# Last layer's values as seven block products over pairs of contexts and pairs of head groups

## The chip, the cores and the metric

One core of a Trainium2 chip runs the whole kernel in one launch. Its engines work side by side, each through its own queue in order: TensorE (PE; PEld is its weight load), VectorE (DVE), ScalarE (ACT), GpSimd (POOL), and SyncE (SP), which issues nearly all transfers (DMAs). The metric is the device time of a launch in microseconds, the median of several executions. All data are float32, and a matmul in float32 shows as two matmul instructions ("passes") in the profile.

## The reference

Four layers run over x [8, 112, 512] with a context ctx [8, 375, 512]: one plain cross-attention, two RWKV layers of 32 heads of 16 channels, and a last layer of two cross-attentions and an MLP. What matters here, shortened:

```python
# layers 1 and 2, time mix (then a channel mix)
def step(s, (r_t, k_t, v_t, w_t)):
    a = k_t[..., :, None] * v_t[..., None, :]
    out = einsum('bhi,bhij->bhj', r_t, u * a + s)
    return a + w_t[..., :, None] * s, out
y = scan(step, s0, (r, k, v, w))
m, va = mean and variance of y over each head's 16 channels
x = x + (((y - m) / sqrt(va + 1e-5)) * gn_w + gn_b) * g @ Wo.T
...
# layer 3, twice (i = 1, 2), H = 16 heads of K = 128, t = 375 positions
h  = layer_norm(x)
qh = (h @ wq + bq).reshape(b, 112, H, K)
kh = concat[(ctx @ wk + bk).reshape(b, t, H, K), bias_k]   # 376 positions
vh = concat[(ctx @ wv + bv).reshape(b, t, H, K), bias_v]
p  = softmax(einsum('bqhk,bthk->bhqt', qh, kh) / sqrt(K))
x  = x + einsum('bhqt,bthk->bqhk', p, vh).reshape(b, 112, H * K) @ wo + bo
```

The keys and values of layer 3 depend on the context alone, not on x, so they can be computed at any time.

## The kernel before

The 16 heads of layer 3 are four groups of four heads, so a group's weight is a 512 x 512 matrix (four chunks k of 128 input channels). "Pieces" of work that depend on nothing near by are made by a Python generator, the filler; `fill(n)` takes n pieces of it and so puts their instructions at that place of the program.

**Values.** `values()` is that filler from layer 1 on. For each attention i, head group gr and context b it loads the context (L723, 750 KB) and multiplies its 375 positions, in chunks of 128, 128 and 119, with the group's weight: four matmuls of 512 columns into one PSUM bank (L751; two banks in all). ScalarE copies the result into one of three tiles `v` (L755) and a transfer stores it in DRAM, `vs` (L756). It yields after each two matmuls, so a piece is four passes. Layer 3 loads `vs` back (L961). There are 64 (i, gr, b) of 3 chunks of 4 matmuls of 2 passes, 1536 in all.

**Where the pieces stand.** In the layer norms of layers 1 and 2 (2, 2 and 4 in each half); 9 before the scans; in the scans one piece in steps 1, 5, 9 and 13 of 16, two in the others, 28 in all; 14 in the tail behind the scans; what is left over is taken in layer 3's first norm and before its first attention, where it is chained with the keys of the first pair of contexts (`first_keys`).

**The scans.** `time_mix` goes through 4 blocks of channels with 16 steps each, 64 in a layer, in an order that `manual_schedule` keeps as written for the engines. A step: `spread` starts a load of a row, spread over the partitions (`vj`, three ahead, L498); VectorE multiplies kv = vp * k in PSUM (L595); ScalarE copies the next `vj` to `vp` (`led`, L506 and L507); VectorE runs the recurrence over 904 elements (`st`, L598, three buffers); GpSimd multiplies rs = st * r (L602, eight buffers); TensorE sums rs into a bank `y` four steps at a time (`sums`, L576); then the pieces. `vp`, `kv` and `y` have one buffer each in PSUM. Beside the steps of one block runs the group norm of the block before, one operation a step: `take` adds y (L544) from step 3; for each half (448 columns) centring by a matmul (L519), square and copy on ScalarE (L522, L523), variance by a matmul (L526), square root (L529), reciprocal on VectorE (L531), products on GpSimd (L533, L539), from steps 4 and 8. Its two matmuls use the banks that the pieces use too.

**Keys.** `attention` computes the keys of layer 3 with seven products where the plain way takes eight (`seven`, matmuls at L794), over pairs of contexts and halves of a group's channels. The sums of contexts that this needs come from layer 0: `context_sums` makes them on GpSimd and stores them for each pair. The attention of a context then takes scores (L967), softmax, transposed probabilities (L970), and probabilities times values (L980, three chunks).

Of the kernel before, what the change touches and what calls it, by code (L numbers as in the profile page):

```python
# [30 lines left out]
P = 128  # L31
# [14 lines left out]
CHUNKS = [(0, 128), (128, 128), (256, T - 256)]  # L46
# [59 lines left out]
def tile_kernel(ctx: ExitStack, tc: tile.TileContext, d: dict, out: bass.AP):  # L106
# [53 lines left out]
    def layer_norm_half(ps, work, y, h, scale, offset, name, room=None, bank=None):  # L160
# [18 lines left out]
        fill(2)  # L179
# [3 lines left out]
        fill(2)  # L183
        var = over_channels(sq, "var")
        fill(4)
# [9 lines left out]
    def layer_norm(ps, work, dst, scale, offset, name, room=None, bank=None):  # L195


        for h in range(2):
            layer_norm_half(ps, work, halves(dst, h), h, scale, offset, name, room, bank)
# [13 lines left out]
    def layer0():  # L213
# [3 lines left out]
        CT = 125  # L217
        with (
# [18 lines left out]
            def context_sums(b, c1, c2):  # L237

                t = work.tile([P, 4, 2, S], F32, tag="sums", name=f"sums0_{b}", bufs=1)
                nc.gpsimd.tensor_sub(t[:, 0], c2[:, :2], c1[:, :2])  # L240
                nc.gpsimd.tensor_sub(t[:, 1], c2[:, 2:], t[:, 0])
                nc.gpsimd.tensor_sub(t[:, 2], c2[:, 2:], c2[:, :2])
                nc.gpsimd.tensor_sub(t[:, 3], c1[:, 2:], t[:, 1])
                to = shared["spill"].tile([P, 2, NC, S], F32, name=f"sums_{b // 2}")
                nc.sync.dma_start(to.rearrange("p a (b k) s -> p (a b) k s", k=2), t)
                shared["sums", b // 2] = to
# [34 lines left out]
            for b in range(B):  # L281
# [4 lines left out]
                if b % 2:  # L286
                    context_sums(b, cxs.pop(b - 1), cxs.pop(b))
# [39 lines left out]
    def rwkv(n, ones_t, center_h, pick, first, state0):  # L327
        pre, names = f"L{n}_xattn_", _RWKV[n]
        with tc.tile_pool(name=f"r{n}", bufs=1) as keep:
# [11 lines left out]
            def gates(name):  # L341
                return keep.tile([P, N], F32, tag="gate", name=name, bufs=2)

            time_mix_inputs(n, pre, names, ones_t, first, k, v, r, g, gates, decay, rows)
            time_mix(n, pre, center_h, pick, state0, k, v, r, g, gates, decay, rows)
        channel_mix(n, pre, names, first)

    def time_mix_inputs(n, pre, names, ones_t, first, k, v, r, g, gates, decay, rows):

        order = names["order"]  # L350
        with (
# [8 lines left out]
            w2e = one.tile([DM, C], F32, name=f"maa2e_{n}")  # L360
# [3 lines left out]
            d2 = one.tile([DD, C], F32, name=f"d2_{n}")  # L364
# [10 lines left out]
            for h in range(2):  # L375
                xa = one.tile([P, NC, NH], F32, tag="xa", name=f"xa{n}_{h}")
                sx = one.tile([P, NC, NH], F32, tag="sx", name=f"sx{n}_{h}")
                layer_norm_half(ps, work, xa, h, pre + "ln1_w", pre + "ln1_b", f"ln1_{n}")
# [3 lines left out]
                for c in range(NC):  # L382
                    nc.vector.scalar_tensor_tensor(
                        xx[:, c, :], sx[:, c, :], vec(pre + "maa_x", c), xa[:, c, :], ALU.mult, ALU.add
                    )
                t4 = one.tile([P, NH], F32, tag="t4", name=f"t4_{n}_{h}")
                t1 = one.tile([DM, NH], F32, tag="t1", name=f"t1_{n}_{h}")
                for dst, m0, m in ((t4, 0, P), (t1, P, DM)):
                    p = mm(ps, f"ps_t{n}_{h}_{m0}")[:m, :NH]
                    for c in range(NC):  # L390
                        nc.tensor.matmul(
                            p, w1[:, c, m0 : m0 + m], xx[:, c, :], start=c == 0, stop=c == NC - 1
                        )
                    nc.scalar.activation(dst, p, AF.Tanh)
# [18 lines left out]
                td = one.tile([DD, NH], F32, tag="td", name=f"td{n}_{h}")  # L413
# [13 lines left out]
                for f, dst, func in (  # L427
# [6 lines left out]
                    for o in range(NC):  # L434
# [5 lines left out]
                        if f == "g":  # L440
                            e = gates(f"g{n}_{o}_{h}")[:, :NH]
# [31 lines left out]
    def time_mix(n, pre, center_h, pick, state0, k, v, r, g, gates, decay, rows):  # L473
# [7 lines left out]
        ps = shared["ps"]  # L481
        mean_h = center_h[1]
        with (
            tc.tile_pool(name=f"s{n}", bufs=1) as one,
            tc.tile_pool(name=f"sw{n}", bufs=2) as work,
            tc.tile_pool(name=f"sv{n}", bufs=1, space=PSUM) as psv,
        ):
            y = v
            order = [4 * q + r for r in range(4) for q in range(4)]
# [3 lines left out]
            def spread(at):  # L493
                if at < len(steps):
                    c, j = steps[at]
                    vjs[c, j] = work.tile([P, N], F32, tag="vj", name=f"vj{n}_{c}_{j}", bufs=3)
# [13 lines left out]
            def gate(c):  # L510
                t = gates(f"gate{n}_{c}")
                nc.sync.dma_start(t, g[:, c, :])
                return t

            def group_norm(c, h, g):

                yh = halves(y[:, c, :], h)
                p = mm(ps, f"ps_gm{n}_{c}_{h}")[:, :NH]
                nc.tensor.matmul(p, center_h[0], yh, start=True, stop=True)  # L519
                yield  # L520
                sq = work.tile([P, NH], F32, tag="sq", name=f"gsq{n}_{c}_{h}")
                nc.scalar.activation(sq, p, AF.Square)  # L522
                nc.scalar.copy(yh, p)  # L523
                yield
                p = mm(ps, f"ps_gv{n}_{c}_{h}")[:, :NH]
                nc.tensor.matmul(p, mean_h, sq, start=True, stop=True)  # L526
                yield
                rstd = work.tile([P, NH], F32, tag="sq", name=f"grs{n}_{c}_{h}")
                nc.scalar.activation(rstd, p, AF.Sqrt, bias=eps)  # L529
                yield  # L530
                nc.vector.reciprocal(rstd, rstd)  # L531
                yield
                nc.gpsimd.tensor_mul(yh, yh, rstd)  # L533
                yield
                nc.scalar.activation(
                    yh, yh, AF.Identity, bias=gn[:, 1, c : c + 1], scale=gn[:, 0, c : c + 1]
                )
                yield
                nc.gpsimd.tensor_mul(yh, yh, halves(g, h))  # L539
# [7 lines left out]
            def beside(c):  # L547
# [4 lines left out]
                return {3: take(c - 1), 4: group_norm(c - 1, 0, g), 8: group_norm(c - 1, 1, g)}  # L552

            for at in range(3):
                spread(at)
            w_o = wpool.tile([P, NC, C], F32, tag="w", name=f"w_{pre}Wo")
            for q in range(4):
                nc.sync.dma_start(
                    w_o[32 * q : 32 * (q + 1)], turned_rows(d[pre + "Wo"].rearrange("p c n -> p (c n)"), q)
                )  # L560
            gn = one.tile([P, 2, NC], F32, name=f"gn{n}")
# [4 lines left out]
            fill(9)  # L566
            waiting, pys = [], {}

            def sums():

                for h in range(2):
                    for c, j, rs in waiting[:4]:
                        if c not in pys:
                            pys[c] = psv.tile([P, 2, 512], F32, tag="y", name=f"ps_y{n}_{c}")
# [12 lines left out]
            with tc.manual_schedule(engines=ORDERED):  # L587
                vp = led(0)
                for c in range(NC):
                    side = beside(c)  # L590
                    for at, j in enumerate(order):
# [3 lines left out]
                        nc.vector.tensor_mul(flat(kv), flat(vp), flat(k[:, c]))  # L595
                        vp = led(c * HS + at + 1)
                        st = work.tile([P, B, LP], F32, tag="st", name=f"st{n}_{c}_{j}", bufs=3)
# [3 lines left out]
                        rs = work.tile([P, N], F32, tag="rs", name=f"rs{n}_{c}_{j}", bufs=8)  # L601
                        nc.gpsimd.tensor_mul(by_batch(rs), st[:, :, :L], by_batch(r[:, c, :]))  # L602
                        waiting.append((c, j, rs))
                        if len(waiting) == 6:
                            sums()
                        fill(1 if at % 4 == 1 else 2)
# [7 lines left out]
            last = gate(NC - 1)  # L614
            last = [group_norm(NC - 1, h, last) for h in range(2)]
            for at in range(10):
                for h in range(2):
                    if at >= 2 * h:
                        next(last[h], None)
                fill(1)  # L620
# [7 lines left out]
    def channel_mix(n, pre, names, first):  # L628
        with (
# [4 lines left out]
            f_k, f_v, f_r = (weight(pre + names[f]) for f in ("Fk", "Fv", "Fr"))  # L634
            xc = one.tile([P, NC, N], F32, name=f"xc{n}")
            sx = one.tile([P, NC, N], F32, name=f"sxc{n}")
            layer_norm(ps, work, xc, pre + "ln2_w", pre + "ln2_b", f"ln2_{n}")
            shifted(sx, xc, first[:, 0])
# [542 lines left out]
```

## Time and profile before

| what | value |
|---|---|
| runs | 3078.76, 3079.95, 3086.07 us; median 3079.95 |
| profiled execution, its own time | 3069.73 us |
| its span, first to last instruction | 3068.0 us |
| mean granted TensorE clock | 0.991 |
| layers 0 and 1 up to the first kv of the scans | 375.46 us, PE busy 356.62 |
| layer 1's scans, 375.46 to 616.16 | 240.70 us, PE 233.27, DVE 220.56, ACT 113.62, POOL 133.38, DMA share 0.85 |
| tail, channel mix, up to layer 2's first kv at 1009.80 | 393.64 us, PE 384.61 |
| layer 2's scans, 1009.80 to 1249.10 | 239.30 us, PE 230.57, DVE 220.31, ACT 113.03, POOL 133.33, DMA share 0.87 |
| tail and channel mix of layer 2, to 1418.00 | 168.90 us, PE 163.85 |
| layer 3, from 1418.00 | 1650.00 us, PE 1611.45, DVE 911.46, DMA share 0.32 |

A row is a stretch of the profiled execution: how long it is and how long each engine was busy in it. Where an engine's busy time comes near the length, it sets the pace or works in step with the one that does. The DMA share is the mean busy share of the 16 DMA engines.

### The profile page before, as it was taken

The numbers are of one execution on the slowest core, as the hardware profiler recorded it, in microseconds if no ns is written. First come the engines' busy times: TensorE is split into PE (matmuls) and PEld (weight loads), VectorE is DVE, ScalarE is ACT, GpSimd is POOL, SyncE is SP. The second block draws the span as 40 slices with busy tenths as digits, with TensorE's granted clock in tenths as the row PEclk, the third lists the DMA queues.
The fourth block names the chain that finished last, engine by engine and source line by source line (L and its number), as shares of the span: only waits on it lengthen the run. The fifth ranks groups of instructions, "written<-read, shape, count | busy, mean of one in ns | idle before, by whom it ended". The sixth has DMA issues, their size and how long they took to land.

```text
span 3068.0 us, 28497 instructions
## 1 busy us (share of the span) xinstructions
PE 2980.4 (97%) x10098; PEld 1575.5 (51%) x10098; DVE 1641.4 (54%) x2432; ACT 812.5 (26%) x1675; POOL 647.3 (21%) x578
## 2 busy tenths in 40 slices
PE   9999999999999999999999999999999999999999
PEld 5634433344444333444366565656566665656544
DVE  1433289933332799454146564655756565645555
ACT  2122245422221444222122121212222221312311
POOL 2222255511322455212000101020001001010030
PEclk9999999999999999999999999999999999999999
DMA  5221398731121888323243342424323343422110
GB/s 226 85 87 61 123 299 252 234 111 65 53 73 66 264 276 259 115 75 116 101 138 131 116 137 96 146 94 137 112 100 125 115 138 104 149 93 91 48 55 24
DMA packets 113149, 390.29 MB, mean 127 GB/s; under 512 B 13112, under 2 KB 20952, under 8 KB 104688
## 3 DMA queue, kind: packets, MB, share of 16 engines
q1 hardware_dynamic: 113008, 388.48, 38.1%
q8 instruction: 80, 1.31, 0.2%
q14 instruction: 61, 0.50, 0.1%
HBM read 320.27 MB, written 68.16 MB: 127 GB/s over the span
## 4 chain that ended last, share of the span: by engine, by line
PE 59%; DVE 4%; issue 1%; DMA 1%; ACT 1%; POOL 0%; SPq 0%; DVEq 0%; ACTq 0%; POOLq 0%
PE ps_v L751 8%; PE av L980 5%; PE ps_k5k L794 5%; PE sc L967 5%; PE ps_k7k L794 5%; PE ps_k1k L794 5%; PE ps_k6k L794 3%; PE pt L970 2%; PE ps_k7q L794 2%; PE ps_k5q L794 2%; PE ps_o L155 2%; PE ps_k7o L794 1%; PE ps_k1q L794 1%; PE ps_k5fc L794 1%; PE ps_k5o L794 1%; PE ps_k7fc L794 1%
## 5 line engine op out<-in xcount | busy, mean ns | idle before, releaser
L751 PE MATMUL ps_v<-wv,cxv 128*128 128x512 f32 (+1 forms) x1536 | 686.6, 599 | 20.3 <-DMA cxv<-in_ctxT 12.4
L751 PEld LDWEIGHTS ps_v<-wv,cxv 128*128 128x128 f32 (+1 forms) x1536 | 284.8, 189 | 406.5 <-issue 371.3
L207 ACT ACTIVATE prob<-sc,top 112x376 f32<-112x376 f32 (+1 forms) x264 | 151.6, 575 | 666.4 <-DVE top L204 543.4
L602 POOL TENSOR_TENSOR rs<-st,r 128x896 f32<-128x896 f32 x128 | 246.6, 1926 | 244.6 <-DVE st L598 193.1
L598 DVE TENSOR_TENSOR_SCAN st<-decay,kv 128x904 f32<-128x904 f32 x128 | 260.7, 2037 | 13.3 <-DVE kv L595 0.5
L967 PE MATMUL sc<-k,q 128*112 128x376 f32 x512 | 202.2, 487 | 3.2 <-ACT q L927 2.4
L980 PEld LDWEIGHTS av<-pts,v 128*128 128x128 f32 (+1 forms) x1536 | 184.8, 193 | 31.2 <-DVE pts L976 16.0
L980 PE MATMUL av<-pts,v 128*128 128x112 f32 (+1 forms) x1536 | 188.7, 277 | 1.6 <-DMA v<-vs 1.6
L794 PE MATMUL ps_k1k<-cx,w_L_xattn_wk 128*128 128x375 f32 x512 | 186.1, 479 | 1.6 <-ACT rstdk L812 1.6
L755 ACT COPY v<-ps_v 128x512 f32<-128x512 f32 (+1 forms) x192 | 111.9, 583 | 259.3 <-PE ps_v L751 234.1
L595 DVE TENSOR_TENSOR kv<-vp,k 128x904 f32<-128x904 f32 x128 | 141.5, 1105 | 60.1 <-ACT vp L507 48.0
L958 POOL COPY k<-vecs 128x4 f32<-128x4 f32 x64 | 12.4, 201 | 742.9 <-PE sc L967 662.1
L204 DVE TENSOR_REDUCE top<-sc 112x1 f32<-112x376 f32 (+1 forms) x264 | 143.5, 544 | 29.2 <-PE sc L967 15.5
L794 PEld LDWEIGHTS ps_k1k<-cx,w_L_xattn_wk 128*128 128x128 f32 x512 | 95.1, 190 | 62.8 <-issue 2.0
L507 ACT COPY vp<-vj 128x896 f32<-128x896 f32 x128 | 116.5, 910 | 35.6 <-DMA vj<-rows 32.0
L209 DVE TENSOR_SCALAR prob<-prob,total 112x376 f32<-112x376 f32 (+1 forms) x264 | 121.2, 462 | 7.7 <-PE ps_k1k L794 0.5
L970 PEld LDWEIGHTS pt<-ident,prob 112*128 112x128 f32 (+1 forms) x768 | 84.7, 140 | 72.1 <-DVE prob L209 44.2
L970 PE MATMUL pt<-ident,prob 112*128 112x112 f32 (+1 forms) x768 | 110.2, 264 | 4.2 <-DVE prob L209 3.5
L987 DVE TENSOR_TENSOR ctxt<-av,bv 128x448 f32<-128x448 f32 x64 | 40.0, 624 | 127.7 <-PE av L980 127.6
L967 PEld LDWEIGHTS sc<-k,q 128*112 128x112 f32 x512 | 78.9, 176 | 44.3 <-ACT prob L207 6.8
L822 DVE TENSOR_TENSOR u2k<-ps_k6k,rstdk 128x375 f32<-128x375 f32 x64 | 35.0, 546 | 121.3 <-PE ps_k6k L794 121.2
L794 PE MATMUL ps_k7k<-cs,wsk 128*128 128x375 f32 x256 | 94.4, 481 | 0.9 <-DVE k L889 0.9
(349 smaller groups left out, 4434.0 us busy)
## 6 DMA issues: line engine op xcount, KB each, us to landing
vj<-rows SPq DMA_DIRECT2D x128, 448.0 KB
cxv<-in_ctxT SPq DMA_DIRECT2D x64, 750.0 KB
cs<-sums SPq DMA_DIRECT2D x64, 750.0 KB
vs<-v SPq DMA_DIRECT2D x128, 256.0 KB
v<-vs SPq DMA_DIRECT2D x64, 512.0 KB
cx<-in_ctxT SPq DMA_DIRECT2D x40, 750.0 KB
vs<-v SPq DMA_DIRECT2D x64, 238.0 KB
v<-vs SPq DMA_DIRECT2D x64, 238.0 KB
```

Of the source, the lines that this page charges most:

```text
L204: nc.vector.tensor_reduce(top, scores, AX.X, ALU.max, negate=True)
L207: nc.scalar.activation(prob, scores, AF.Exp, bias=top, accum_out=total)
L209: nc.vector.tensor_scalar(prob, prob, total, None, ALU.mult)
L507: nc.scalar.copy(vp[:, :, 1:], by_batch(vjs.pop((c, j))))
L595: nc.vector.tensor_mul(flat(kv), flat(vp), flat(k[:, c]))
L598: nc.vector.tensor_tensor_scan(flat(st), flat(decay[:, c]), flat(kv), 0.0, ALU.mult, ALU.add)
L602: nc.gpsimd.tensor_mul(by_batch(rs), st[:, :, :L], by_batch(r[:, c, :]))
L751: nc.tensor.matmul(p, cx[:, k, t0 : t0 + m], w_v[:, k, :], start=k == 0, stop=k == NC - 1)
L794: nc.tensor.matmul(p, lhsT, right[:, k], start=start and k == 0, stop=k == 1, skip_group_check=not start)
L967: nc.tensor.matmul(sc, q[:, o, tok], kt[:, o, :], start=True, stop=True)
L970: nc.tensor.transpose(pt[t][:nt, o, :], prob[:, t0 : t0 + nt], ident[:L, :L])
L980: nc.tensor.matmul(av[:, o, :], v[:nt, t, o * HD : (o + 1) * HD], pts[:nt, t, o, :], start=t == 0, stop=t == 2,)
```

## The change

The values are made by seven products of 256 input channels where the plain way takes eight. With a pair of contexts (positions of one chunk) and a pair of head groups, the context has blocks c11, c21 (halves of the channels of the first) and c12, c22 (of the second), the weights a11, a12 (halves for the first group) and a21, a22. The products are k1 = a11 c11, k2 = a12 c21, k6 = s1 t1, k7 = s2 t2, k8 = a22 t3, k5 = (a21 + a22) t0 and k9 = s3 c22, with sums t of the contexts and s of the weights; k1 + k2, k1 + k6 + k7 + k8, k1 + k6 + k7 + k5 and k1 + k6 + k5 + k9 are the four results.

**Chained in a bank.** k6, k7 and k8 are added to k1 in its PSUM bank, and ScalarE copies the bank out after each of the four; k2 has the other bank and is added to k1 by GpSimd; k5 and k9 are chained in the other bank in the middle of the next unit, and VectorE adds them (`last_two`). A unit (one chunk of 125 positions of a pair) has the order k1, k5 and k6, k9 and k7, k2, k8, with k5 and k9 of the unit before. There are four sets (i, pair of groups) of 12 units, and a fifth set of 3 units that makes keys: groups 1 and 2 of the first attention for the first pair of contexts, stored in DRAM and loaded in `key_pieces`. One product, four passes of 512 columns (16 of 125 for keys), is a piece.

```diff
-CHUNKS = [(0, 128), (128, 128), (256, T - 256)]
+CT = S // 3
+CHUNKS = [(0, CT), (CT, CT), (2 * CT, CT + 1)]
+BLOCKS = 7
+UNITS = B // 2 * 3
...
+        sets = [("wv", i, (gr, gr + 1)) for i in (1, 2) for gr in (0, 2)] + [("wk", 1, (1, 2))]
+        units = [(at, unit) for at in range(len(sets)) for unit in range(UNITS if at < 4 else 3)]
+        def tile_of(name):
+            return pool.tile([P, C], F32, tag="v", name=name, bufs=6)
...
+        def block(at):
+            m = at // 2
+            if m + 4 not in tiles:
+                load(m + 4)
+            return tiles[m][:, at % 2]
...
+        def last_two(u, f, u2, u3, s, at):
+            p = bank(u, f, f"k5_{u}")
+            product(p, block(at), s["k5"])
+            nc.vector.tensor_add(u3, p, u3)
+            store(u3, u, 1, 1)
+            yield "k5"
+            product(p, block(at + 2), s["k9"], start=False)
+            nc.vector.tensor_add(u2, p, u2)
+            store(u2, u, 0, 1)
+            yield "k9"
...
+            for what, n in (("k1", 0), ("k6", 2), ("k7", 4)):
+                product(first, block(base + n), s[what], start=not n)
+                kept.append(shaped(tile_of(f"{what}_{u}"), f))
+                nc.scalar.copy(kept[-1], first)
+                after(what)
+                yield
+                if n < 4:
+                    yield from late()
+            p1, u2, u3 = kept
+            p = bank(u + 1, f, f"k2_{u}")
+            product(p, block(base + 5), s["k2"])
+            y = shaped(pool.tile([P, C], F32, tag="k2", name=f"k2_{u}"), f)
+            nc.scalar.copy(y, p)
+            nc.gpsimd.tensor_add(p1, y, p1)
+            store(p1, u, 0, 0)
+            after("k2")
+            yield
+            product(first, block(base + 6), s["k8"], start=False)
+            y = shaped(tile_of(f"k8_{u}"), f)
+            nc.scalar.copy(y, first)
+            store(y, u, 1, 0)
+            after("k8")
+            yield
+            before = last_two(u, f, u2, u3, s, base + BLOCKS + 1)
```

**Blocks and weights.** Layer 0's `park` takes the place of `context_sums`: it makes the seven blocks of each pair and chunk (ScalarE copies three, GpSimd makes four sums) and stores them in DRAM in the order in which they will be read. `block` loads them two at a time, four loads ahead, into five tiles. `weights` loads a set's four blocks and makes the three sums on GpSimd; for three of the sets `relay` does this piece by piece in the last two units of the set before, each tile when its last use is past. The keys of layer 3 load their context sums from the same blocks.

**In the scans.** Two pieces a step, one of them before `vp`, but only one in steps 6 and 10 (30 in 16 steps); `st` has two buffers, `rs` six; the first two `vj` have a place of their own (`early`). The group norm works on both halves at once in the banks of `y`, its reciprocals come in four parts, `take` at step 2, centring at 3, variance at 4, reciprocals at 5, 6, 9 and 10. Pieces in the norms: none in the first half of layer 1's, two fewer in the second half of the channel mixes', three more after `xx`; 8 before the scans; in the tail 4 and then 5 in layer 1, 4 and 11 in layer 2; after the channel mix's norm 7 in layer 1 and all that are left in layer 2.

```diff
                         nc.vector.tensor_mul(flat(kv), flat(vp), flat(k[:, c]))
+                        fill(1)
                         vp = led(c * HS + at + 1)
-                        st = work.tile([P, B, LP], F32, tag="st", name=f"st{n}_{c}_{j}", bufs=3)
+                        st = work.tile([P, B, LP], F32, tag="st", name=f"st{n}_{c}_{j}", bufs=2)
...
                         waiting.append((c, j, rs))
+                        fill(int(at not in (6, 10)))
                         if len(waiting) == 6:
                             sums()
-                        fill(1 if at % 4 == 1 else 2)
...
             layer_norm(ps, work, xc, pre + "ln2_w", pre + "ln2_b", f"ln2_{n}")
+            fill(7 if n == 1 else 1000)
```

**Layer 3.** The pools of the values are closed before it, and its own are opened. The filler of its norms is the keys of the first pair alone. The keys are left without their bias, which shifts all scores of a query alike, except that the bias position's key becomes bias_k - bk (`over`). The values' tiles have 126 rows, 125 positions and the bias. State and small constants of the RWKV layers are loaded where they are used, and two small weights share a tile.

```diff
-        filler = chain(filler, first_keys())
+        filler = first_keys()
...
+            if ("wk", i, gr, b) in shared:
+                for j in range(2):
+                    kts.append(kv.tile([P, HG, T], F32, tag="kt", name=f"k{u}_{j}", bufs=3))
+                    for t in range(3):
+                        y = shared["wk", i, gr, b + j][:, t]
+                        nc.sync.dma_start(kts[-1][:, :, t * CT : (t + 1) * CT], y)
+                return
...
-                nc.gpsimd.tensor_copy(kt[:, :, S], vecs[:, at : at + HG])
+                nc.gpsimd.tensor_copy(kt[:, :, S], over[:, gr * HG : (gr + 1) * HG])
```

## The prediction

> **What bounds the kernel now.** I read the page's busy times, its slices and its costliest groups first, then windows cut at the 16-step blocks of the scans, then the vector and tensor timelines inside them.
>
> ```profile
> PE 2980.4 (97%) x10098; PEld 1575.5 (51%) x10098; DVE 1641.4 (54%) x2432; ACT 812.5 (26%) x1675; POOL 647.3 (21%) x578
> ...
> PE   9999999999999999999999999999999999999999
> ...
> DVE  1433289933332799454146564655756565645555
> ...
> DMA  5221398731121888323243342424323343422110
> ...
> L751 PE MATMUL ps_v<-wv,cxv 128*128 128x512 f32 (+1 forms) x1536 | 686.6, 599 | 20.3 <-DMA cxv<-in_ctxT 12.4
> ```
>
> TensorE is busy in every slice; only 3068.0 - 2980.4 = 87.6 us of the span are idle. So a removed matmul pass is worth its time wherever something else doesn't take over. One thing nearly does: in slices 5 to 7 and 13 to 15, the two scans, VectorE is at 8 or 9 tenths too, and so is the DMA.
>
> ```profile
> 446.30:507.70 61.40, 60.34 (x189) 24.31 (x188) 56.83 (x36) 30.72 (x56) 35.22 (x20) 1.00 0.81 242
> 507.70:567.40 59.70, 57.18 (x180) 22.53 (x178) 56.69 (x36) 27.90 (x52) 35.19 (x20) 1.00 0.84 258
> ...
> 1009.80:1079.80 70.00, 65.84 (x196) 26.12 (x195) 62.73 (x40) 30.72 (x58) 36.57 (x19) 0.98 0.96 290
> ```
>
> Columns: length, busy PE, PEld, DVE, ACT, POOL, granted clock, DMA share, GB/s. A block of 16 steps takes 59.7 to 61.4 us with VectorE busy 56.7: two engines are full at once.
>
> ```profile
> 487.80 1.11 DVE L595 TENSOR_TENSOR kv<-vp,k 128x904 f32<-128x904 f32 x1
> 489.01 2.04 DVE L598 TENSOR_TENSOR_SCAN st<-decay,kv 128x904 f32<-128x904 f32 x1
> 491.15 1.11 DVE L595 TENSOR_TENSOR kv<-vp,k 128x904 f32<-128x904 f32 x1
> ...
> 505.77 2.04 DVE L598 TENSOR_TENSOR_SCAN st<-decay,kv 128x904 f32<-128x904 f32 x1
> 507.73 1.06 DVE L544 TENSOR_TENSOR v<-ps_y,v 128x896 f32<-128x896 f32 x1
> 508.71 1.10 DVE L595 TENSOR_TENSOR kv<-vp,k 128x904 f32<-128x904 f32 x1
> ...
> 525.27 2.93 DVE L531 RECIPROCAL grs<-grs 128x448 f32<-128x448 f32 x1
> 528.12 1.08 DVE L595 TENSOR_TENSOR kv<-vp,k 128x904 f32<-128x904 f32 x1
> ```
>
> A bare step is 491.15 - 487.80 = 3.35 us: 1.11 + 2.04 and two gaps of 0.1, because each instruction needs the one before. What is slipped in between fills such a gap: the add of 1.06 us moves the next kv from 507.91 (505.77 + 2.14) to 508.71, so it costs 0.80, 0.26 under its length; a reciprocal costs 2.66.
>
> ```profile
> 1485.99 44.37 PE L751 MATMUL ps_v<-wv,cxv 128*128 128x512 f32 x103
> ...
> 706.72 1.62 PE L155 MATMUL ps_fk<-xk,w_L_xattn_fWk_None 128*128 128x448 f32 x2 [2.14 <-DVE xk L644]
> ...
> 1023.95 7.08 PE L751 MATMUL ps_v<-wv,cxv 128*128 128x512 f32 x12 [3.83 <-DMA cxv<-in_ctxT]
> ```
>
> The first line gives the price of a pass of 512 columns: 44.37 / 103 = 0.431 us, so a piece (4 passes) is 1.72. It also shows values left over and run bare in layer 3.
>
> **1. Tensor work: -74.** The 64 value matrices cost 1536 passes. Seven products of 4 passes for each of 4 pairs of head groups x 4 pairs of contexts x 3 chunks are 48 x 28 = 1344. 192 x 0.431 = -82.7. Added: keys of two groups for the first pair of contexts, 3 units x 7 x 16 = 336 passes of 125 columns. No such pass is shown; 24 passes of 112 columns take 2.93 us (L308), 0.122 each, and a weight load takes 0.190 (L794). Bounds 41 and 64; I take 0.13, near the first row because loads of 0.19 are hidden beside passes of 0.122 there: +43.7. The same keys leave layer 3: 2 x 56 passes of 375 columns at 0.315 (four in 1.26, 1549.41 to 1550.67): -35.3. Sum -74.3.
>
> **2. The scans get longer: tensor idle +21.** A step now holds two pieces, 30 in 16 steps (one is left out at steps 6 and 10) where there were 28. Each unit of 7 pieces brings 2 adds from PSUM on VectorE, 125x512. Rows: 448 columns 0.62 (L987), 896 columns 1.06; between them 0.69, less 0.26 for the gap: 0.43 (bounds 0.29, from 375 columns at 0.546, and 0.80). The reciprocals come as four halves instead of two wholes, 4 x (1.47 - 0.26) = 4.8 against 5.3.
> A later block on VectorE: 16 x 3.35 + 8.6 adds x 0.43 + 0.8 + 4.8 = 62.9 us. On TensorE: 30 x 1.72 + four groups of sums x 1.71 + centring and variance 4 x 0.92 = 62.1. Balanced over the block, but not within it. From step 13 to step 5 TensorE has all but one of the extras (sums at 13, 1 and 5; centring at 3, variance at 4): 9 x 3.45 + 8.8 = 39.8 us against VectorE's 9 x 3.35 + 2.1 + 0.8 = 33.1. From 6 to 12 VectorE has the reciprocals and TensorE two skipped pieces: 29.9 against 22.5. If neither could run ahead, a block would be 39.8 + 29.9 = 69.7. How far they can: the chained banks let TensorE go one product past an unfinished add, 1.72 - 0.69 = 1.0 us; for the pieces that ScalarE copies out, about 2. So 67.7 to 68.7; the recips at 5 already start beside the last sums, which gives up to 1.2 back. I take 67.5. The first block has no such extras: VectorE 57.3, TensorE 56.7, lumps of 1.7: I take 59.5. A layer: 59.5 + 3 x 67.5 = 262 us, of which TensorE works 56.7 + 3 x 62.1 = 243: idle 19, twice 38. Before, by the windows from the first kv to the last scan, it idled 7.5 and 8.8. +21 (bounds +5, if the halves of a block overlap wholly, and +30).
>
> **3. New waits behind the copies: +8.** ScalarE's copy of the first piece of a step now stands ahead of vp, and the next kv waits for vp. Each unit takes four of six v buffers, so the k8 copy takes the one whose store was issued three products (5.2 us) earlier; before, the copies of six products lay between. A vj issued at 378.83 reached vp at 387.71, 8.9 us, at DMA share 0.97; in later blocks the share is 0.73 to 0.88. Bytes per step grow by one piece more of 268 KB against 249, 8% over a step 8% longer, so the share stays. Bounds 0 and 34 units x 1.7 = 58; I take 8, since at the later share ScalarE lost only 0.2 us to stores. GpSimd's two new kinds of work (an add of 512 columns a unit, about 1.27, and relays of weights at about 2.5, twice the 1.27 to 1.70 that 512 columns take at L769 to L772, 5 a set) lie in its idle time: 35 of 60 us are used in a block. With st down to two buffers its scan partner has 2.7 us to spare (next scan but one), so one relay fits; if two meet, a scan waits some 2 us.
>
> **4. Idle elsewhere: -12.** Pieces are put where TensorE waits today: 6.05 + 2.81 at the first norm (150 to 161), 2.14 + 0.89 + 0.31 at 707, 2.73 + 0.40 at 804, 1.27 at 913, 4.0 at 1340, 4.87 at 1422: 25 us. Layer 3's norm now has keys as filler, whose adds stand in VectorE's chain there. Half: -12 (bounds 0 and -25). The context blocks, weight sums in layer 0, state0 loaded per layer and the stored keys' loads cost nothing while the DMA share is 0.2 to 0.6 there and nothing waits; uncovered, the keys' 1.5 MB would cost 6 us once at 250 GB/s. The first two vj have buffers of their own, so the scan can start up to 3 us sooner a layer; TensorE has pieces there either way.
>
> **Sum.** -74.3 + 21 + 8 - 12 = -57. The profiled execution took 3069.7 us (span 3068.0) and becomes 3012; the median of the runs, 3079.95, is 10.2 us above it: 3080 - 57 = 3023.
>
> [...] Here the 70 us with the 3.83 us gap ran at 0.98, and those with gaps under 2 us at 1.00. [...]
>
> **The rivals.** *Full gain:* VectorE absorbs the adds and the scans stay tensor-bound, with as little tensor idle as today, and no copy waits: -74 - 12 = -86, 2994. For it: both engines total 62 to 63 a block. Against: the order of the lumps. *Stores late:* ScalarE waits 1 us in each of the 34 units for a store to land: -57 - 8 + 34 = -31, 3049. For it: the 8.9 us landing and the halved distance. Against: blocks are read in pieces of 250 KB, not 750, so less is queued ahead. *Slower:* one mechanism, in the scans: an add stands in VectorE's queue behind a whole scan, TensorE can't enter the chained bank until it's done, and the later product then holds the next scan. 68 adds x 2.04 us = 139 in place of part 2 and 3: -74 - 12 + 139 = +53, 3133. It decides from 86 / 68 = 1.27 us an add on. For it: VectorE is 93% busy there and in order. Against: the one-product slack above. *No change:* the value work that is saved was cover in front of waits (tails, norms), so that it comes back as idle; 3080. Against: 34 pieces run bare at 1486 to 1544, and tails and norms keep 9 to 21 pieces.
>
> **How the numbers follow.** Forecast 0.50 (own range 3005 to 3042), full gain 0.14, stores late 0.19, no change 0.06, slower 0.11. A measurement here can tell 0.3%, 9 us, from no change. Faster: 0.50 + 0.14 + 0.19 = 0.83; same 0.06; slower 0.11. The range goes from 2985 (full gain with bare passes at their low bounds) to 3068 (stores late at twice the wait) and leaves out the slower case and the middle of no change, 0.17.
>
> **What would show it.** ps_v passes 1344 + 336 and PE busy near 2906. kv steps of 3.35 plus 0.4 at an add; blocks of 67 us with VectorE busy 62; tensor idle of 2 to 3 us after steps 5 and 9 whose releaser is an add; vector waits at steps 1 to 5. No values after the second scans' channel mix; layer 3 shorter by about 59 + 35 us. Wrong if the blocks pass 72 us, if ScalarE's copies wait for stores, or if norms and tails grow idle.

## The result, and the profile after

The changed kernel takes 3296.09 us (median of 4 runs, 3290.1 to 3299.07) against 3079.36 (4 runs): 1.07 times as long, 95% interval 1.0674 to 1.0726. Forecast were 3023 us and a range up to 3068. The profiled execution has a span of 3297.3 us and a mean granted clock of 0.951, where 0.991 was granted before.

The page after, the same lines as before the change and the group that is new among the waits; below it, that group in the page of before:

```profile
PE 3022.1 (92%) x10130; PEld 1632.8 (50%) x10130; DVE 1688.8 (51%) x2532; ACT 842.0 (26%) x1754; POOL 768.3 (23%) x668
...
PE   8989998898999998899899898998899899998899
...
DVE  0433288756223588843555454545645454544555
...
DMA  6312377743202677642233333333232333323110
...
L1170 PE MATMUL av<-pts,v 125*128 125x112 f32 (+1 forms) x1536 | 232.6, 317 | 113.6 <-DMA v<-wvs 113.6
```

```profile
L980 PE MATMUL av<-pts,v 128*128 128x112 f32 (+1 forms) x1536 | 188.7, 277 | 1.6 <-DMA v<-vs 1.6
```

TensorE now idles 3297.3 - 3022.1 = 275.2 us in place of 87.6, and most of its slices of 8, of which there were none, lie in the scans and all over layer 3. The two long lines name the largest part: probabilities times values wait 113.6 us for the load of the values, 1.6 before, and a pass of theirs takes 317 ns where it took 277.

The windows of layer 1's four blocks of 16 steps (columns as in the prediction):

```profile
403.77:471.00 67.23, 61.05 (x164) 22.93 (x165) 55.05 (x42) 28.12 (x53) 34.82 (x20) 0.95 0.77 239
471.00:541.80 70.80, 66.30 (x192) 25.87 (x191) 61.54 (x46) 33.75 (x62) 43.19 (x26) 0.95 0.75 232
541.80:622.30 80.50, 67.59 (x192) 25.88 (x191) 61.21 (x46) 32.77 (x62) 46.01 (x28) 0.94 0.77 237
622.30:694.97 72.67, 64.86 (x191) 24.73 (x189) 61.09 (x45) 31.56 (x60) 41.36 (x25) 0.98 0.67 210
```

Blocks take 67 to 80.5 us, not 59.5 and 67.5. VectorE's 61 are near the 62 that were forecast; neither it nor TensorE fills the block. The DMA share went down, from 0.85 and 0.87 over the two scans to 0.74 and 0.75, and yet ScalarE waits for transfers and VectorE behind it (us in all, times, longest):

```profile
ACT vp L539 <- DMA vj<-rows: 84.5, 45, 6.4
...
ACT k L912 <- DMA wvs<-k: 22.6, 20, 2.4
...
DVE kv L637 <- ACT vp L539: 63.2, 34, 14.2
```

The second line is a copy that waits until the store of its buffer has landed. Before, copies waited 0.2 us for stores, and ScalarE less than half as long for `vj`:

```profile
ACT vp L507 <- DMA vj<-rows: 32.0, 17, 4.4
```

In layer 3, one load of values and its use, from the timeline:

```profile
2073.30 0.28 SPq L1152 DMA_DIRECT2D v<-wvs  x1
...
2083.12 4.53 PE L1170 MATMUL av<-pts,v 125*128 125x112 f32 x24 [3.30 <-DMA v<-wvs]
```

The load is issued at 2073.30 and TensorE can start at 2083.12; the 24 passes behind it take 4.53 us where an undisturbed group takes 2.83; the clock records have a granted 0.5 from 2083.9 to 2087.3. By the trace's packet records this load of 125 rows of 6 KB lands after 7.8 us. (A landing time here is a median, to the end of the last packet; where a load is cut into several transfers, all their times count from the issue of the last one, which comes 0.3 to 0.7 us behind the first.) Before, 128 rows of 4 KB landed after 2.9 and the 119 rows of 2 KB behind them after 4.3.

The trace's clock records have 13 stretches at half rate (granted 0.5), 55.6 us together, before; 62 stretches, 321.1 us, after, 174.3 of them in layer 3 (11.2 before). These sums hold a last stretch each, of 1.0 and 0.2 us, that begins just behind the last instruction and costs nothing; so do those of e1, e4 and e6 below, with 1.4 to 1.6 us. After the change TensorE has 30 waits over 1.5 us for the values; in 27 of them, or at most 1.5 us behind, a stretch at half rate begins.

### The profile page after: what moved, and what is told of

It reads as the page before. It is cut to its first block, busy times and chain, and to the rows that moved or that the text cites. A ratio compares the mean times of both kernels' runs of the same rounds, so it can differ in the third digit from the quotient of the medians.

```text
span 3297.3 us, 29544 instructions
## 1 busy us (share of the span) xinstructions
PE 3022.1 (92%) x10130; PEld 1632.8 (50%) x10130; DVE 1688.8 (51%) x2532; ACT 842.0 (26%) x1754; POOL 768.3 (23%) x668
## 4 chain that ended last, share of the span: by engine, by line
PE 42%; DMA 9%; DVE 2%; issue 1%; ACT 1%; POOL 0%; ACTq 0%; DVEq 0%; POOLq 0%
DMA v<-wvs 9%; PE av L1170 7%; PE ps_k5k L973 4%; PE ps_k7k L973 4%; PE sc L1157 4%; PE ps_k1k L973 3%; PE ps_k7q L973 2%; PE ps_k5q L973 1%; PE ps_k6k L973 1%; PE ps_k7o L973 1%; PE pt L1160 1%; PE ps_k1q L973 1%; PE ps_k5o L973 1%; PE ps_k5fc L973 1%; PE ps_k7fc L973 1%; PE ps_k6q L973 1%
## 5 line engine op out<-in xcount | busy, mean ns | idle before, releaser
L834 PE MATMUL ps_vk<-wv,cv 128*125 128x512 f32 x1336 | 633.9, 620 | 76.2 <-ACT k L912 19.4
L834 PEld LDWEIGHTS ps_vk<-wv,cv 128*125 128x125 f32 x1336 | 249.0, 193 | 440.7 <-issue 303.1
L1170 PE MATMUL av<-pts,v 125*128 125x112 f32 (+1 forms) x1536 | 232.6, 317 | 113.6 <-DMA v<-wvs 113.6
L1170 PEld LDWEIGHTS av<-pts,v 125*128 125x128 f32 (+1 forms) x1536 | 229.3, 232 | 153.6 <-issue 141.0
L1150 POOL COPY k<-over_k 128x4 f32<-128x4 f32 x64 | 15.8, 252 | 795.0 <-PE sc L1157 726.7
L973 PE MATMUL ps_k1k<-cx,w_L_xattn_wk 128*128 128x375 f32 x480 | 177.6, 483 | 2.2 <-ACT rstdk L991 2.2
L206 DVE TENSOR_REDUCE top<-sc 112x1 f32<-112x376 f32 (+1 forms) x264 | 143.4, 544 | 28.9 <-PE sc L1157 14.8
L912 ACT COPY k<-ps_vk 125x512 f32<-125x512 f32 (+1 forms) x153 | 89.0, 582 | 184.3 <-PE ps_vk L834 156.5
L539 ACT COPY vp<-vj 128x896 f32<-128x896 f32 x124 | 112.8, 910 | 87.2 <-DMA vj<-rows 84.5
L1160 PEld LDWEIGHTS pt<-ident,prob 112*125 112x125 f32 (+1 forms) x768 | 97.6, 175 | 63.7 <-DVE prob L211 38.0
L1160 PE MATMUL pt<-ident,prob 112*125 112x112 f32 (+1 forms) x768 | 116.4, 273 | 4.5 <-DVE prob L211 4.5
L923 POOL TENSOR_TENSOR k<-k,k 125x512 f32<-125x512 f32 (+1 forms) x51 | 67.4, 1321 | 144.0 <-ACT k L922 128.6
```

Source lines behind the costliest of these rows:

```text
L206: nc.vector.tensor_reduce(top, scores, AX.X, ALU.max, negate=True)
L539: nc.scalar.copy(vp[:, :, 1:], by_batch(vjs.pop((c, j))))
L834: nc.tensor.matmul(to, left[:, k], right[:, k], start=start and n == 0, stop=k == 1, skip_group_check=True)
L973: nc.tensor.matmul(to, lhsT, rhs, start=start and k == 0, stop=k == 1, skip_group_check=not start)
L1160: nc.tensor.transpose(pt[t][:nt, o, :], prob[:, t0 : t0 + nt], ident[:L, :L])
L1170: nc.tensor.matmul(av[:, o, :], v[:nt, t, o * HD : (o + 1) * HD], pts[:nt, t, o, :], start=t == 0, stop=t == 2,)
```

## The experiments

Theory A: the number of rows of a transfer decides over how many of the 16 DMA engines it goes. The change made all stores and loads of values 125 rows, where they had been 128 (and 119 for the last chunk). The rival for the scans is the lock of VectorE and TensorE over the adds, the slower case of the prediction; for layer 3, that one transfer of 750 KB, or the blocks' loads in packets of 1000 bytes, takes so long.

**Four cuts of the transfers.** The first cuts layer 3's load by rows:

```diff
-                nc.sync.dma_start(v[:CT], shared["wv", i, gr, b][:CT])
+                nc.sync.dma_start(v[:112], shared["wv", i, gr, b][:112])
+                nc.sync.dma_start(v[112:CT], shared["wv", i, gr, b][112:CT])
```

> The changed kernel with the value load of layer 3 cut by rows, 112 and 13, in place of one transfer of 125 rows. Theory A: the number of rows decides over how many DMA engines a transfer goes, and 125 rows go over few; the load then lands some 3 to 4.5 us after its issue in place of 7.8, TensorE's 113.6 us of waits for it fall under 20, and with them go most of the half-clock windows of layer 3 (174 us of them). Layer 3 loses 113.6 - 20 + (174 - 20) / 2 = about 170 us: time near 3125, and the scans stay at 67 to 80 us a block. Theory B (the load is late because 750 KB in one transfer, or loads of blocks in 1000-byte packets ahead of it, take that long): landing and time stay, 3290.

Measured: 3124.24 us (one run). The load lands after 4.3 us, layer 3 has 35.5 us at half rate, and of the 113.6 us of waits one is left:

```profile
PE av L1171 <- DMA v<-wvs: 3.0, 1, 3.0
```

Cut by chunks in place of rows:

```diff
+                nc.sync.dma_start(v[:CT, :2], shared["wv", i, gr, b][:CT, :2])
+                nc.sync.dma_start(v[:CT, 2], shared["wv", i, gr, b][:CT, 2])
```

> The changed kernel with the same load cut by chunks, as before the change: chunks 0 and 1 of all 125 rows, then chunk 2 of all 125 rows. Theory A (the number of rows decides): both transfers still go over few engines, the second lands about when the one did, 7.5 to 9 us, and the time stays within 20 us of 3296. Theory B (one transfer of 750 KB is what is slow): first part lands near 3 us as before the change, the second near 4.3, and the time falls towards 3125.

Measured: 3223.51 us (one run), which neither theory had. The landing times are those of A, 5.3 us for the first part and 7.4 for the second; what A's expectation left out is that TensorE starts on the first part when that has landed, so that it waits 48.8 us for the values and 17.0 for the bias row behind them. That is 47.8 us less than 113.6, and 61.6 us fewer at half rate are worth at most 30.8: 78.6, measured 72.6 (65.3 of the span lie behind layer 2's scans).

The stores, layer 3 as it is, and then both:

```diff
-            nc.sync.dma_start(where[: y.shape[0], unit % 3], y)
+            cuts = (0, 112, CT) if y.shape[0] == CT else (0, P)
+            for a, z in zip(cuts, cuts[1:]):
+                nc.sync.dma_start(where[a:z, unit % 3], y[a:z])
```

> The changed kernel with the stores of the values cut by rows, 112 and 13, layer 3 as it is. Theory A (in the scans the stores of 125 rows fill a few DMA engines, and the loads of vj, which need all of them, queue there): ScalarE's 84.5 us of waits for vj fall under 25, VectorE's 63 us for vp likewise, blocks fall from 67 to 80 us to 62 to 68, and the two scans lose 40 to 80 us together: time 3215 to 3255. Rival (VectorE's adds and the chained banks lock VectorE and TensorE, as my slower case had it): blocks stay at 71 to 76, time within 15 us of 3296.

> Both loads and stores cut by rows, 112 and 13. Theory A: the gains of the two runs add up, 170 + 60: time near 3065, between 3030 and 3095; that is, about where the kernel before is or below. Rival (lock of VectorE and TensorE in the scans, load late for another reason): 3230 to 3296.

Measured: 3216.32 us for the stores alone (one run). The blocks (layer 1, windows) and ScalarE's wait:

```profile
395.75:456.45 60.70, 57.71 (x162) 22.22 (x163) 54.93 (x41) 28.17 (x53) 34.31 (x20) 0.97 0.91 270
456.45:524.25 67.80, 64.84 (x194) 25.89 (x193) 61.39 (x47) 34.02 (x62) 43.26 (x26) 0.97 0.82 236
524.25:591.95 67.70, 62.27 (x192) 24.95 (x191) 61.04 (x46) 33.08 (x62) 46.44 (x28) 1.00 0.85 248
```

```profile
ACT vp L539 <- DMA vj<-rows: 10.5, 11, 2.9
```

The same bytes, by more transfers, at a higher DMA share, and the wait for `vj` is 10.5 us in place of 84.5. With both cut: 3065.28 us (10 runs), ratio to before 0.997 (0.9953 to 0.9986). Alone the two gains are 172 and 80, together 231, 21 less than their sum: of e3's 80, some 24 lie behind the scans, where the load's wait came out shorter too (104.2 us in place of 113.6), a part that e1 gains as well.

**One row moved.** In its sharp form theory A supposes that the number of engines is a divisor of the number of rows. To test that, e4's load was cut at 113, a prime:

```diff
-                nc.sync.dma_start(v[:112], shared["wv", i, gr, b][:112])
-                nc.sync.dma_start(v[112:CT], shared["wv", i, gr, b][112:CT])
+                nc.sync.dma_start(v[:113], shared["wv", i, gr, b][:113])
+                nc.sync.dma_start(v[113:CT], shared["wv", i, gr, b][113:CT])
```

> e4 with the cut of layer 3's value load moved by one row: 113 and 12 rows in place of 112 and 13. Theory A in its sharp form (a transfer goes over as many engines, up to 16, as divide its number of rows: 112 over 16, 125 over 5, 113, a prime, over one): the load lands near 113 x 0.286 = 32 us after its issue in place of 4.3; with one buffer for 64 contexts layer 3 gets longer by 64 x 10 to 64 x 25 us, 640 to 1600: time 3700 to 4700. Rival (two smaller transfers are what helped): lands at 4.3 as in e4, time 3060 to 3080.

Measured: 4209.23 us (one run); the load lands after 29.2 us (median), 4.3 with 112. TensorE's waits:

```profile
PE av L1173 <- DMA v<-wvs: 982.5, 56, 25.5
```

One row costs 1144 us. The time for a row fits one engine: (29.2 - 0.6) / 113 = 0.25 us, against (7.8 - 0.9) / 25 = 0.28 for 125 rows over five; a packet of 6 KB, one row, took 0.23 us after the change (median).

The packet records don't name an engine, but they show how many packets of this load are under way at once: five in 80% of the time that any is after the change; 16 more often than any other number (35%) in e4; one in 97% in e9. Before, the loads of layer 3 had 16 more often than any other number (26%) with 128 rows, and seven (31%) with 119. What other numbers of rows do is not shown. About a quarter of the 125-row stores in the scans are issued before the one ahead has landed, and yet no more than five of their packets are under way in 97% of the time, which fits five engines that all of them share.

**The rows of the change in the kernel before.** The first cuts its load of 128 rows, the second its stores of 128 rows, into 125 and 3:

```diff
-                nc.sync.dma_start(v[:, :2], shared[i, gr, b][:, :2])
+                nc.sync.dma_start(v[:125, :2], shared[i, gr, b][:125, :2])
+                nc.sync.dma_start(v[125:, :2], shared[i, gr, b][125:, :2])
...
-                nc.sync.dma_start(to[:m, t], v)
+                cuts = (0, 125, m) if m > 125 else (0, m)
+                for a, z in zip(cuts, cuts[1:]):
+                    nc.sync.dma_start(to[a:z, t], v[a:z])
```

> The kernel before the change with the first part of its value load (512 KB, 128 rows of 4096 bytes) cut into 125 and 3 rows; nothing else. Theory A (125 rows go over 5 DMA engines, 25 rows each, where 128 go over 16): the first part lands near 25 x 0.2 + 0.6 = 5.6 us after its issue in place of 2.9, the second near 7 in place of 4.3; TensorE's waits for it, 1.6 us now, become 40 to 90, half-clock windows come to layer 3, and the kernel gets slower by 50 to 150 us: 3125 to 3225. Theory B (what costs in the changed kernel is something else of the change, such as the packets of the blocks' loads): within 15 us of 3073.

> The kernel before the change with its stores of 128 rows cut into 125 and 3 rows, loads as they were. Theory (stores of 125 rows fill 5 of the 16 DMA engines in the scans, so that vj lands late): 9 such stores a block here against 17 in the changed kernel, ScalarE's wait for vj grows from some 32 us to 45 to 90, blocks of 60 become 61 to 66, time 5 to 45 us above the kernel before. Rival (it is the number of stores and of packets, not their rows): no growth beyond 5 us.

Measured: 3137.99 us for the load (before: 3076.13 beside it), landings 5.1 and 6.6 us; 3114.13 for the stores (3074.34), one run each. The waits, of the first by TensorE and of the second by ScalarE:

```profile
PE av L981 <- DMA v<-vs: 37.1, 26, 3.5
...
PE av L981 <- DMA v<-overs: 8.5, 11, 1.6
```

```profile
ACT vp L507 <- DMA vj<-rows: 121.0, 68, 5.5
```

Without any of the change's arithmetic, both losses appear; the waits for the load, 37.1 us, stay under the 40 to 90 that were expected, those for `vj`, 121.0, go beyond their 45 to 90.

**What is left in e4.** The adds of k5 and k9 leave VectorE (k9 likewise):

```diff
-            nc.vector.tensor_add(u3, p, u3)
+            z = shaped(pool.tile([P, C], F32, tag="k2", name=f"zk5_{u}"), f)
+            nc.scalar.copy(z, p)
+            nc.gpsimd.tensor_add(u3, z, u3)
```

> Loads and stores cut as in e4; k5 and k9 are copied out by ScalarE and added by GpSimd in place of VectorE's adds. Theory (part 2 of the prediction: the adds lengthen VectorE's side of a block and keep TensorE out of the chained bank, 28.9 us of waits for them in e4): blocks of 66.5 to 72 become 63 to 68, time 3065 less 15 to 45: 3020 to 3050. Rival (GpSimd has no room: its add of 1.3 us stands before rs, st has two buffers, the scan waits): blocks stay or grow, 3060 to 3090.

Measured: 3052.03 us (4 runs), ratio to before 0.992 (0.9893 to 0.9947). Two blocks of layer 1:

```profile
455.50:519.90 64.40, 62.41 (x194) 25.24 (x193) 56.88 (x38) 39.05 (x71) 51.07 (x33) 1.00 0.83 239
519.90:588.20 68.30, 62.94 (x194) 25.08 (x193) 56.89 (x38) 37.30 (x70) 60.50 (x39) 1.00 0.87 256
```

VectorE falls from 61 to 57 us a block and the scans lose 14.3 us (522.5 against 536.8); the time is 13 us under e4's, a little short of the 15 to 45 that were expected. The second block suggests why, with GpSimd at 60.5 of 68.3 us; no run shows it.

Then layer 0, whose first layer norm starts at 156 us in place of 149. Four tries: the block copies go to GpSimd (e7); on e6, the blocks' stores too, onto GpSimd's queue (e10), and the first weights are loaded ahead of the blocks, k6's sum made second (e11); on e11, the turning of Wv and Wg goes to GpSimd alone (e13):

```diff
-                        nc.scalar.copy(y[:, k], z[:, k])
+                        nc.gpsimd.tensor_copy(y[:, k], z[:, k])
...
-                    nc.sync.dma_start(
+                    nc.gpsimd.dma_start(
...
-            nc.gpsimd.tensor_add(a21, a21, a22)
-            nc.gpsimd.tensor_sub(s1, a21, a11)
+            nc.gpsimd.tensor_sub(s1, a22, s2)
+            nc.gpsimd.tensor_add(a21, a21, a22)
...
-                        nc.scalar.copy(t, w)
+                        nc.gpsimd.tensor_copy(t, w)
```

> Loads and stores cut as in e4; layer 0's three block copies of each pair moved from ScalarE to GpSimd. Theory (they stand in ScalarE's queue behind 8.1 us of waits for the blocks' store, and TensorE's results of q and w_vo can't be copied out behind them): the first kv comes 8 to 14 us earlier than in e4 (397.0), time 3051 to 3057. Rival (other work of layer 0 sets its end): first kv and time stay within 3 us.

> e6 with layer 0's block copies on GpSimd and the stores of the blocks issued from GpSimd's queue in place of SyncE's. Theory (in e7 the load of Wv still stands on SyncE's queue behind 9.6 us of block stores, the copies that turn Wv wait for it on ScalarE, and w_vo's copies behind them hold TensorE for 4.65 us): that wait goes, the first layer norm starts near 149 as before the change in place of 156, time 3052 less 5 to 12: 3040 to 3047. Rival (the end of layer 0 is set by something else, or issuing from GpSimd holds up its own sums): first layer norm at 154 to 157, time 3047 to 3060.

> e10 and the first set of weights loaded ahead of the blocks, with the sum that k6 needs made second in place of third. Theory (TensorE waits 8.5 us for these loads and 3.2 for the sum before it can go on with layer 1's norm): waits 3 to 6 us shorter, time 3 to 6 us under e10. Rival (the transfers share the same engines, the order changes nothing): within 2 us of e10.

> e11 with the copies that turn Wv and Wg (a pair of copies for each block, ScalarE's first and GpSimd's second) made by GpSimd alone. Theory (in e7 and e10 the wait of 4.5 to 4.7 us only moved: ScalarE's part of the turning waits, once for the load of Wv, once for GpSimd's queue, and the copies of w_vo or q stand behind it): TensorE has no wait over 1 us between 10 and 150 us, the first layer norm starts at 147 to 150 in place of 156, and the time is 5 to 9 us under e11's 3050: 3041 to 3045. Rival (GpSimd becomes late for the blocks or the weights): first layer norm at 153 or later, 3048 to 3060.

Measured: 3066.74 us for e7 (10 runs), 3054.18 for e10, 3050.14 for e11 (4 runs each), 3058.17 for e13 (6 runs). The norm starts at 156.1, 155.5, 156.1 and 156.4: the theories of e7, e10 and e13 about layer 0 fell. Each removed wait came back at the next engine, as TensorE's lines from the timelines of e7, e10 and e13 show:

```profile
66.67 9.90 PE L286 MATMUL ps_w_vo<-w_L_xattn_w_o_None,t_v 128*128 128x512 f32 x16 [4.65 <-ACT w_vo L289]
```

```profile
57.82 1.97 PE L276 MATMUL ps_tv<-ident,w_L_xattn_w_v_None 128*128 128x128 f32 x8 [4.52 <-ACT q L299]
```

```profile
91.91 0.58 PE L324 MATMUL pt<-ident,prob 112*125 112x112 f32 x3 [3.26 <-DVE prob L211]
```

What sets the end of layer 0 stays open; it is about 7 us. With the reordered weights of e11 TensorE's wait for them falls from 9.9 us to 3.1 and the one for the sum (2.9) is gone, as expected; the time is 4 us better than e10's by the medians, less than the runs tell apart. e11 is the fastest of all versions, 0.9914 of before (0.9896 to 0.9933), and e6, simpler, can't be told from it.

## Why the prediction was wrong, by its steps

Stages of the profiled executions, us, cut at the first kv and the last scan of each layer:

| stage | before | after | e4, rows cut | e6 |
|---|---|---|---|---|
| to layer 1's first kv | 375.5 | 403.8 | 397.0 | 394.4 |
| scans of layer 1 | 240.7 | 291.2 | 263.0 | 257.9 |
| between | 393.7 | 412.2 | 406.1 | 404.6 |
| scans of layer 2 | 239.2 | 294.1 | 273.8 | 264.6 |
| rest | 1818.9 | 1896.1 | 1726.7 | 1728.8 |
| span | 3068.0 | 3297.3 | 3066.6 | 3050.3 |
| at half rate, in all | 55.6 | 321.1 | 117.7 | 100.3 |

The step that failed is not in the sum: the prediction gave the value transfers of layer 3 no term, and covered those of the scans with "Bytes per step grow ... so the share stays". In its place the runs show transfers of 125 rows with five packets or fewer under way at once (94% of the time for the load, 97% for the stores), as over 5 of the 16 engines. Cutting the rows alone takes 230.7 us of span off the changed kernel: 169.4 in the rest (layer 3), 48.5 in the scans, 12.8 elsewhere.

**1, tensor work, -74: right.** e4's TensorE is busy 2932.6 us. With half of the 62.1 us more at half rate taken as lost to a slower clock, 31.1, that leaves 2901.5, 78.9 under before; as not all of that half need be lost, 78.9 is an upper bound. The groups say the same more directly: layer 3's keys fall from 648.4 us to 612.1, -36.3; the stored keys' 320 recorded passes take 39.4 us, 0.123 each, so their 336 take 41.4; with the prediction's -82.7 for 192 passes the sum is -77.6. The rest behind layer 2's scans is 92.2 us shorter in e4, forecast 59 + 35.

**2, scans: right in the main, once the stores are out of the way.** e4's blocks are 61.3, 66.5, 68.0, 67.3 in layer 1 and 65.0, 69.6, 66.9, 72.3 in layer 2, forecast 59.5 and 67.5, so that both scans take 536.8 us, not 524, and the last block passes the 72 that the prediction set as a sign of being wrong. TensorE idles 33.9 us in both scans where it idled 16.1, +17.8 against +21, and 21.9 of the 33.9 are waits for the adds of k5 and k9, as part 2 has it. Taking the adds off VectorE (e6) leaves 26.3 us of the idle time.

**3, waits behind copies and stores, +8: too small, and without its larger half.** It looked for v copies that wait for a free buffer. They came, 22.6 us where 0.2 were before, and with the stores cut (e4) they are 5.2. The larger harm was to others, the loads of `vj` with 84.5 us, which the prediction took to go on as before: from 471 to 695 us of the changed kernel the trace has 6423 packets of 2 KB at 91 ns (mean), which over five engines is 117 us on each of them; `vj`, blocks and the rest, if they go evenly over all 16, add 126. By this estimate from the records the five have 243 us of work in 224 us, the other eleven are busy 56%, and `vj`, of which up to 16 packets are under way at once (more in 0.1% of the time), would land when the fullest engine is done. The mean share over 16 engines shows 0.73 and hides it. "Stores late", the rival at 3049, had the place and the wait, but 34 us instead of 48.5, nothing for `vj` and nothing for layer 3.

**4, idle elsewhere, -12: wrong.** Outside the scans TensorE idles 71.5 us before and 100.1 in e4, +28.6. Fewer pieces stand before the scans, and new waits are among them: 8.8 us for the first weights' load and 3.2 for GpSimd's sum of them, where the prediction had the weight sums of layer 0 cost nothing, then 9.2 us at layer 3's first norm, where 4.9 were waited before.

**The clock: the row was the wrong one to go by.** The prediction's row is one 70 us stretch at 0.98, which has 3.41 us at half rate in the records, and its sum has no term for the clock. Half rate grew by 265.5 us after and by 62.1 in e4. At most half of that is lost: a stretch of 3.4 us lengthened the group of 24 passes shown above by 1.70 us, but a row of 32 passes in layer 1 (below) by 0.82. In e4 that makes at most some 31 us, which part 1 takes off the busy time and the sum puts back. With all four, -78.9 + 31.1 + 17.8 + 28.6 = -1.4, e4's span against before. Of the forecast's -57, part 4 thus lost 40.6 (+28.6 against -12) and the clock up to 31.1; parts 1 to 3 gave some 16 back.

The trace of before had the sign. Its second value load, 238 KB in 119 rows, took from 2.25 to 4.33 us after its issue, 117 GB/s; the first, 512 KB in 128 rows, from 0.59 to 2.91 on the same scale, 226 GB/s. A packet of 2 KB took 84 ns and one of 4 KB 159 (medians), so the packets' size alone doesn't make the difference. The first most often had 16 packets under way at once, the second seven. The change gives every transfer of values a number of rows that, like the second's, isn't 128.

The slower rival (adds lock VectorE and TensorE) gave the sign and not the cause: TensorE waits 29.3 us for the adds of k5 and k9 after the change and 28.9 in e4, not 139.

## What to carry to other kernels

When an edit changes a tile's number of rows, look at each load and store of it: the load of 125 rows had five packets under way at once in 80% of the time and landed after 7.8 us, cut at 112 it had 16 more often than any other number and landed after 4.3, and the fix is a cut in the transfer, not in the arithmetic. A falling mean DMA share together with growing waits for loads can mean that a few engines are full, as by the estimate above: in the scans the share fell from 0.85 and 0.87 to 0.74 and 0.75 while the waits for `vj` grew from 32.0 us to 84.5. TensorE's waits for the values cost more than themselves: in e1, 110.6 us of them less, with 138.8 us less at half rate in layer 3, were worth 172 us.

## What the runs showed of the hardware that was not expected

The half-rate stretches, but for each trace's last one, are 3.41, 6.83 or 10.24 us long and start whole multiples of 3.413 us apart, in both kernels (after: 28.0, 35.0, 40.0, 43.0, 49.0 of them behind the first). Some of them follow no idle time at all. After the change, layer 1:

```profile
230.38 3.27 PE L432 MATMUL ps_mv<-t,maa 32*128 32x448 f32 x8
233.58 13.99 PE L464 MATMUL ps_v<-xv,w_L_xattn_Wv_None 128*128 128x448 f32 x32
247.50 3.27 PE L432 MATMUL ps_mr<-t,maa 32*128 32x448 f32 x8
```

TensorE is busy without a gap, yet 3.4 us at half rate begin at 233.9 and at 251.0, each as a group of eight passes with 32 of 128 rows ends; the 32 passes behind take 13.99 us where they took 13.17 in the kernel before (from 213.34). The two are 17.1 us apart, five times 3.413, so that the slowed sequence meets a multiple of 3.413 us at the same place again; at full clock, as before the change, it is 16.29 long and drifts away from it. In layer 2 the kernel before has the same at 935.6, 952.7 and 969.8, and none in layer 1. That the few rows cause it is an inference from where the stretches lie; no run changed them. Executions of the same code up to layer 3 (e4, e9) reach the first kv at 397.0 and 391.1 us, with 37.5 and 20.5 us at half rate before it and the same idle time of TensorE (32.2 and 32.1 us): by the granted 0.5, up to half of the 17 us between them, 8.5, can be the clock's alone, and the two lie 5.9 us apart.
